# A graph network's edge loop on one core: every tile gathered, no column copies, one-hot weights by whole-group operations

## The chip, the cores and the metric

The kernel runs on one core of one Trainium2 chip. The core has five engines with instruction streams of their own: TensorE (PE, matrix products; PEld in the profile is its weight load), VectorE (DVE), ScalarE (ACT), GpSimd (POOL) and SyncE (SP, which here issues DMAs). They meet by semaphores. The metric is the device time of one execution in microseconds: 3987.03 us before the change, the median of three runs (3986.22 to 3988.06).

## The reference

One layer of attention over a graph's edges with 12,500 nodes of 64 features and 412,500 edges (400,000 and a loop for each node), sorted by receiver (dst); all in float32:

```python
h = jnp.maximum(_layernorm(x, axis=-1), 0.0)
msg_in = jnp.concatenate([h[src], h[dst], edge_attr_32], axis=-1)      # 64 + 64 + 32
messages = swish(msg_in @ W1 + b1) @ W2 + b2
att = softmax(swish(msg_in @ Wa1 + ba1) @ Wa2 + ba2, axis=0)           # over all edges
aggregated = segment_sum(messages * att, dst, num_segments=12500)
x = x + swish(concat([h, aggregated]) @ Wu1 + bu1) @ Wu2 + bu2
```

The softmax runs over all edges at once, so its maximum and its sum are known only at the end.

## The kernel before, in words

**Head.** `gnn_kernel` loads x in chunks, normalizes it, transposes it into hT (two halves of the nodes on 128 partitions), and multiplies it with the sender's and the receiver's halves of the first weights. The results are two tables in DRAM of 128 numbers per node: ts_d for senders (L274), tr_d for receivers (L310). The first gather needs all of ts_d.

**Edges.** 128 edges make a tile, K = 8 tiles make a group, and there are NG = 403 groups. `one_pass` goes over the groups. In `load(g)`, two groups ahead, GpSimd gathers the senders' rows of each tile with one indirect DMA per tile (L533) into a buffer gs, of which there are seven. SyncE loads the edge features, the receivers' numbers and a window of the receivers' table, VectorE makes one-hot columns from the receivers' numbers (L558), and four matmuls (L562) give the receivers' and the edges' share in PSUM (pe).

In 127 groups (`chosen`, every third, without the first ten and the last twelve or so) the eighth tile is not gathered. `numbers` loads its senders' numbers, `places` computes where each sender's column stands in hT (L487 to L493), `columns` copies these 128 columns one by one on ScalarE (L504, with the places in registers), and in `load` a mask (L567) and one more matmul (L568) turn them into the tile's share.

`begin(g)` adds pe and gs on VectorE (L573, written back into gs) and takes the hyperbolic tangent on ScalarE (L576). `end(g)` makes the messages (L586) and the logits (L592 to L597). For each batch of groups `top` and `weigh` update the running maximum, whose history is kept in nmax, and take the exponentials p.

**Sums by node.** Some groups later `sum_up` runs in three steps: `out_of` copies a group's sums out of PSUM (L652, ScalarE), `put` adds an earlier group's into the table sums by node (L671, L675) and notes in the table stand which maximum these sums were made with (L678), and `by_node` makes the weights wt, a one-hot row of 40 columns times p for each edge (L640, eight instructions per group), and multiplies them with the messages (L646). `project` multiplies with the update's weights (L657).

**Beside the loop** `tile_bias` and `tile_rest` make the nodes' own share of the update, one tile of nodes in eight groups; L389 adds a bias to x there.

**Tail.** After the last group the 13 tiles of nodes go through `factor` (an exponential that brings the sums to the last maximum, L830), `first`, `silu`, `second` and `rest`, and are stored. `general` is a second way for graphs whose windows are too wide; it is not taken here.

**Order.** Nearly all instructions are pinned with `pin`, so each engine keeps the order in which the program names them. SyncE, ScalarE and GpSimd issue DMAs in the order of their streams. A gather waits for the gather eight before it to have landed and for its buffer to be free.

Of the kernel before, what the change touches and what calls it, by code (L numbers as in the profile page):

```python
# [44 lines left out]
F32 = mybir.dt.float32  # L45
# [8 lines left out]
P = 128  # L54
EP = 128
# [18 lines left out]
EVERY = 3  # L74
PHASE = 1
SLOTS = (((0, 24), (24, 24)), ((48, 24), (72, 12)), ((84, 24), (108, 20)))
ROUND = 12582912.0
# [3 lines left out]
BIG = 3.0e38  # L81


PARTS = [("pair", 4 * C), ("we", C), ("bias", C), ("wu2h", 2 * D), ("wa2", U), ("bu2", D), ("w_bu", U),
         ("w2b", U), ("wu1a", U), ("wu2", D), ("ba2", 1), ("w_bup", 2 * U), ("bu1", 1)]
# [5 lines left out]
def gnn_kernel(ctx: ExitStack, tc: tile.TileContext, n_edges, x, src, src_row, dst, dst_row, first, edge,  # L91
# [14 lines left out]
    hT_d = dram.tile([2 * D, NB // 2, P], F32, name="hT_d")  # L106
# [19 lines left out]
    w_bu = part["w_bu"][:D + 1]  # L126
# [29 lines left out]
    hT = const.tile([2 * D, NB // 2, P], F32, name="hT")  # L156
# [8 lines left out]
    with tc.tile_pool(name="node1", bufs=1) as node1, \  # L165
# [7 lines left out]
        for c, n in chunks:  # L173
            xc = node.tile([P, CB, D], F32, name="xc", bufs=min(len(chunks), 8))[:, :n, :]
# [138 lines left out]
        pin(nc.scalar.dma_start(hT_d, hT))  # L313
# [6 lines left out]


def node_bias(tc, b, v, work, ps):

    nc = tc.nc
    NB, w_bu = v["NB"], v["w_bu"]
    n = min(4, NB - b)
    hb = work.tile([D + 1, 4, P], F32, name="hb")
    nc.vector.memset(hb[D:, :, :], 1.0)
    for r in range(2):
        nc.sync.dma_start(hb[:D, r:n:2, :], v["hT_d"][r * D:(r + 1) * D, b // 2:(b + n) // 2, :])  # L330
    pb = ps.tile([P, 4, P], F32, name="mt")
    nc.tensor.matmul(pb[:U, :n, :], w_bu, hb[:, :n, :], start=True, stop=True)
    return pb[:U, :n, :]
# [60 lines left out]
def one_pass(tc, n_edges, v):  # L394
# [17 lines left out]
    with ExitStack() as ctx:  # L412
# [5 lines left out]
        stand = keep.tile([P, NH + 2 * W], F32, name="stand")  # L418
# [15 lines left out]
        nc.vector.memset(start[:, 1:2], BIG)  # L434
# [5 lines left out]
        hT = v["hT"].rearrange("d b p -> d (b p)")  # L440
        stack = keep.tile([2 * D, C], F32, name="stack")
        nc.vector.tensor_tensor(stack, v["w_pair"][:, 0, :C], v["w_pair"][:, 0, C:], ALU.add)
        half = keep.tile([P, 1], F32, name="half")
        nc.vector.memset(half[:D], 0.0)
        nc.vector.memset(half[D:], 1.0)
# [10 lines left out]
        with tc.tile_pool(name="work2", bufs=2) as work2, \  # L456
# [3 lines left out]
            pes, gss, lgs, ps_, psums, sps, pps, ees, mts, nums, cols = ({} for _ in range(11))  # L460
# [10 lines left out]

            chosen = {g for g in range(8, NG - 12) if g % EVERY == PHASE}

            def numbers(g):
                if g in chosen:
                    e = (g * K + K - 1) * EP
                    n = nums[g] = small.tile([P, EP], I32, name="num", bufs=2)
                    nc.sync.dma_start(n, bass.AP(tensor=v["src_row"].tensor,
                                                 offset=v["src_row"][:, e:].offset, ap=[[0, P], [1, EP]]))

            def places(g):
                if g not in chosen:
                    return
                n = nums[g]
                near = small.tile([1, EP], F32, name="near", bufs=1)
                to = small.tile([1, EP], I32, name="to", bufs=2)
                pin(nc.vector.tensor_scalar(to, n[0:1], 1, None, op0=ALU.logical_shift_right))  # L487
                m = NB // 2
                pin(nc.vector.tensor_scalar(near, to, 1.0 / m, 0.5 / m - 0.5, op0=ALU.mult, op1=ALU.add))
                pin(nc.vector.tensor_scalar(near, near, ROUND, None, op0=ALU.add))  # L490
                pin(nc.vector.tensor_scalar(near, near, ROUND, float(1 - m * P), op0=ALU.subtract, op1=ALU.mult))
                pin(nc.vector.scalar_tensor_tensor(to, to, float(P), near, op0=ALU.mult, op1=ALU.add))
                pin(nc.vector.tensor_scalar(n, n, 1, None, op0=ALU.bitwise_and))  # L493
                cols[g] = small.tile([P, EP], F32, name="cols", bufs=2), to

            def columns(g, first, n):
                if g not in chosen:
                    return
                to, at = cols[g]
                _, regs = nc.values_load_multi_w_load_instructions(  # L500
                    at[0:1, first:first + n], engines=[ENG.Activation], min_val=0, max_val=NP // 2 - 1,
                    skip_runtime_bounds_check_because=WHY)
                for i in range(n):
                    pin(nc.scalar.copy(to[:, first + i:first + i + 1], hT[:, bass.ds(regs[i], 1)]))  # L504

            def burst(g, k):
                for i in range(EVERY):
                    columns(g + 3 + i, *SLOTS[EVERY - 1 - i][k])

# [14 lines left out]
            def load(g):  # L524
# [6 lines left out]
                for j in range(K - (g in chosen)):  # L531
                    rows = WIDE if j == 3 else EP
                    nc.gpsimd.indirect_dma_start(  # L533
                        out=full[:rows, j, :], out_offset=None, in_=ts_d[:, :],
                        in_offset=bass.IndirectOffsetOnAxis(ap=src_full[:rows, t + j:t + j + 1], axis=0))
# [25 lines left out]
                for q in range(H):  # L561
                    pin(nc.tensor.matmul(pe[:, 2 * q:2 * q + 2, :], eo[:, q * EP:(q + 1) * EP],  # L562
                                         win[:, q // 2, :, :], start=True,
                                         stop=q < H - 1 or g not in chosen))
                if g in chosen:
                    to, _ = cols[g]
                    pin(nc.vector.scalar_tensor_tensor(to, nums[g], half, to, op0=ALU.is_equal, op1=ALU.mult))  # L567
                    pin(nc.tensor.matmul(pe[:, K - 1, :], to, stack, start=False, stop=True))  # L568

            def begin(g):  # L570

                n = K - (g in chosen)
                pin(nc.vector.tensor_tensor(gss[g][:, :n, :], pes[g][:, :n, :], gss[g][:, :n, :], ALU.add))  # L573
                if n < K:
                    pin(nc.vector.tensor_copy(gss[g][:, n, :], pes[g][:, n, :]))
                pin(nc.scalar.activation(pes[g], gss[g], AF.Tanh))  # L576

            def end(g, then=None):
# [4 lines left out]
                gs, th = gss.pop(g), pes.pop(g)  # L583
# [50 lines left out]
            def by_node(g):  # L634
# [4 lines left out]
                for j in range(K):  # L639
                    pin(nc.vector.tensor_scalar(wt[:, j, :], iota_w[:EP, j // H, :],  # L640
                                                dloc[:, g * K + j:g * K + j + 1],
                                                p[:, k + j:k + j + 1],
# [498 lines left out]
```

## Time and profile before

| what | value |
|---|---|
| median of three runs | 3987.03 us |
| the profiled execution | 3986.92 us, span 3985.1 us |
| TensorE busy | 2332.9 us (59%) |
| VectorE busy | 3264.8 us (82%) |
| ScalarE busy | 2173.0 us (55%), 17,477 instructions |
| GpSimd busy | 2950.2 us (74%), 3,122 instructions |
| mean granted clock of TensorE | 0.64 |
| DMA | 391.64 MB, mean 98 GB/s |

The profile is of one execution. A group's row has the line, the engine, the operation, the tiles written and read, the shapes and the count; then the busy time and the mean duration in ns; then how long the engine was idle just before these instructions and what ended that. "issue" there means that the engine waited for nothing that the profile shows. A row of the timeline begins with the start and the duration in us; idle time before it stands in brackets. Rows of windows give each engine's busy time between two times.

### The profile page before, as it was taken

What the parts mean: (1) busy time and instruction counts of PE and PEld (TensorE: products, weight loads), DVE (VectorE), ACT (ScalarE), POOL (GpSimd) and SP (SyncE); (2) the same over time, 40 slices, a digit from 0 to 9 for tenths busy, and PEclk for the clock granted to TensorE, in tenths of its full rate; (3) what the DMA queues carried; (4) which work ended last, traced back from release to release, by engine and by line L of the source; (5) the groups of instructions that cost most, each with busy time, mean ns of one, the idle gap of its engine ahead of it and who ended that gap; (6) DMA issues with size and microseconds to landing.
All of it is one profiled execution on the core that took longest, in us unless ns stands there. A gap on an engine that the chain in (4) does not pass through costs nothing. (4 is left out here: it accounts for less than half of the span.)

```text
span 3985.1 us, 80416 instructions
## 1 busy us (share of the span) xinstructions
PE 2332.9 (59%) x11238; PEld 1888.3 (47%) x11238; DVE 3264.8 (82%) x9553; ACT 2173.0 (55%) x17477; POOL 2950.2 (74%) x3122
## 2 busy tenths in 40 slices
PE   6556566666666555555555555555655555555566
PEld 5444444454444444444444444444544444444455
DVE  6888888888888787888878888887878887878787
ACT  3655555555555555555555555555555555555512
POOL 3777777777777777777777777777777777777774
PEclk8766666666666666666666666666666665666666
DMA  8333343333333333333333333333333333333333
GB/s 287 101 99 99 95 110 92 103 99 102 102 92 95 93 85 93 87 92 88 89 94 84 95 93 86 94 84 94 88 91 94 84 95 87 91 95 84 104 105 85
DMA packets 219778, 391.64 MB, mean 98 GB/s; under 512 B 72209, under 2 KB 146898, under 8 KB 206050
## 3 DMA queue, kind: packets, MB, share of 16 engines
q0 software_dynamic: 99104, 203.16, 19.1%
q1 hardware_dynamic: 118754, 173.60, 16.7%
q10 hardware_dynamic: 1376, 9.67, 0.6%
q14 instruction: 452, 3.70, 0.3%
q8 instruction: 92, 1.51, 0.2%
HBM read 360.42 MB, written 25.72 MB: 97 GB/s over the span
## 5 line engine op out<-in xcount | busy, mean ns | idle before, releaser
L533 POOL DMA_INDIRECT gs<-ts_d,src_sb x3097 | 2933.0, 947 | 992.6 <-issue 854.1
L562 PE MATMUL pe<-wins,eo 128*128 128x256 f32 x3224 | 1465.1, 630 | 925.7 <-DVE eo L558 679.6
L504 ACT COPY cols<-hT 128x1 f32 x16256 | 1605.0, 187 | 717.7 <-issue 714.8
L562 PEld LDWEIGHTS pe<-wins,eo 128*128 128x128 f32 x3224 | 970.9, 318 | 1222.7 <-DVE eo L558 769.0
L576 ACT ACTIVATE pe<-gs 128x1024 f32<-128x1024 f32 x403 | 413.7, 1026 | 928.6 <-DVE gs L573 496.8
L573 DVE TENSOR_TENSOR gs<-pe,gs 128x1024 f32<-128x1024 f32 (+1 forms) x403 | 475.4, 1180 | 393.6 <-DMA gs<-ts_d,src_sb 369.2
L640 DVE TENSOR_SCALAR wt<-iota_w,dloc,p 128x40 f32<-128x40 f32 x3224 | 726.1, 321 | 1.8
L646 PE MATMUL sp<-wt,acts 128*65 128x40 f32 x6448 | 628.8, 268 | 6.3 <-DVE wt L640 3.9
L646 PEld LDWEIGHTS sp<-wt,acts 128*65 128x65 f32 x6448 | 589.9, 183 | 16.2 <-DVE wt L640 9.7
L657 PEld LDWEIGHTS mt<-ss,w2u 65*128 65x128 f32 x806 | 203.0, 279 | 336.2 <-issue 173.9
L657 PE MATMUL mt<-ss,w2u 65*128 65x40 f32 x806 | 181.6, 319 | 242.3 <-DVE gm L623 202.0
L616 PE MATMUL mt<-ident,mx 128*128 128x128 f32 x107 | 47.4, 443 | 445.8 <-DVE sums L675 427.2
L594 DVE TENSOR_TENSOR pe<-pe,w_all 128x512 f32<-128x512 f32 x403 | 281.8, 699 | 13.4
L558 DVE TENSOR_SCALAR eo<-dbs,bj 64x256 f32<-64x256 int32 x806 | 277.9, 375 | 18.2 <-DMA dbs<-in_dst_row_dram 9.0
L592 DVE SCALAR_TENSOR_TENSOR pe<-pe,gs 128x512 f32<-128x512 f32 x403 | 280.3, 696 | 10.5
L586 DVE SCALAR_TENSOR_TENSOR acts<-pe,gs 128x512 f32<-128x512 f32 x403 | 277.2, 688 | 12.4 <-ACT pe L576 3.2
L597 DVE TENSOR_REDUCE lg<-pe 128x8 f32<-128x512 f32 x403 | 277.0, 687 | 10.5
L616 PEld LDWEIGHTS mt<-ident,mx 128*128 128x128 f32 x107 | 19.5, 182 | 456.9 <-issue 455.0
L678 DVE COPY stand<-nmax 64x40 f32 x806 | 161.0, 200 | 3.2
L671 DVE SCALAR_TENSOR_TENSOR sums<-sums,scale,mt 64x40 f32 x214 | 54.2, 253 | 89.2 <-PE mt L657 85.0
L675 DVE TENSOR_TENSOR sums<-sums,mt 64x40 f32 x592 | 111.5, 188 | 4.7 <-PE mt L657 0.6
L357 DVE TENSOR_SCALAR bu<-mt,w_all 64x256 f32<-64x256 f32 (+1 forms) x50 | 23.9, 477 | 88.7 <-PE mt L348 88.3
(124 smaller groups left out, 1062.7 us busy)
## 6 DMA issues: line engine op xcount, KB each, us to landing
eo<-in_edge_dram SPq DMA_DIRECT2D x100, 512.0 KB
dbs<-in_dst_row_dram SPq DMA_DIRECT2D x200, 256.0 KB
gs<-ts_d,src_sb POOLq DMA_INDIRECT x3097
wins<-tr_d SPq DMA_DIRECT2D x806, 32.0 KB
num<-in_src_row_dram SPq DMA_DIRECT2D x127, 64.0 KB
ts_d<-ts SPq DMA_DIRECT2D x5, 896.0 KB
tr_d<-tr ACTq DMA_DIRECT2D x5, 896.0 KB
hT_d<-hT ACTq DMA_DIRECT2D x1, 3136.0 KB
```

The source lines that it names most:

```text
L504: pin(nc.scalar.copy(to[:, first + i:first + i + 1], hT[:, bass.ds(regs[i], 1)]))
L533: nc.gpsimd.indirect_dma_start(out=full[:rows, j, :], out_offset=None, in_=ts_d[:, :], in_offset=bass.IndirectOffsetOnAxis(ap=src_full[:ro ...
L558: pin(nc.vector.tensor_scalar(eo[:WR, e], db[:, e], bj[g // NQ % 2 * WR:(g // NQ % 2 + 1) * WR, g, h:h + 1], None, op0=ALU.is_equal))
L562: pin(nc.tensor.matmul(pe[:, 2 * q:2 * q + 2, :], eo[:, q * EP:(q + 1) * EP], win[:, q // 2, :, :], start=True, stop=q < H - 1 or g not in ...
L573: pin(nc.vector.tensor_tensor(gss[g][:, :n, :], pes[g][:, :n, :], gss[g][:, :n, :], ALU.add))
L576: pin(nc.scalar.activation(pes[g], gss[g], AF.Tanh))
L586: pin(nc.vector.scalar_tensor_tensor(acts[g % ACTS][:, :, 0:U], th[:, :, U:C], 1.0, gs[:, :, U:C], op0=ALU.add, op1=ALU.mult))
L592: pin(nc.vector.scalar_tensor_tensor(att, th[:, :, 0:U], 1.0, gs[:, :, 0:U], op0=ALU.add, op1=ALU.mult))
L594: pin(nc.vector.tensor_tensor(att, att, wa2[:EP, None, :].to_broadcast([EP, K, U]), ALU.mult))
L640: pin(nc.vector.tensor_scalar(wt[:, j, :], iota_w[:EP, j // H, :], dloc[:, g * K + j:g * K + j + 1], p[:, k + j:k + j + 1], op0=ALU.is_equ ...
L646: pin(nc.tensor.matmul(sp, acts[g % ACTS][:, j, :], wt[:, j, :], start=j == 0, stop=j == K - 1))
L657: pin(nc.tensor.matmul(pp, w2u.rearrange("s h u -> s (h u)"), sps.pop(g), start=True, stop=True))
```

## The change

- Every group gathers all eight tiles. `numbers`, `places`, `columns` and `burst` go, with the chosen groups, the input src_row, the mask and the extra matmul. ScalarE is left with tangents, exponentials and a few copies at the start.
- The sum of pe and gs goes into a buffer of its own, sm (two of them), and gs is no longer needed after that.
- The one-hot weights of a group are made by two instructions on all eight tiles, an is_equal and a multiplication, rather than by eight on one tile each.
- The copy in `out_of` goes from ScalarE to VectorE.
- stand keeps one number per node and half on 32 partitions rather than on 64, and lies in a common buffer hS with hT, in the part where the chunks of x are at the start. In the tail `factor` spreads it over the 128 partitions with a matmul with a constant matrix pick, and takes the exponential in place.
- The copy of hT to DRAM goes; the general way takes the nodes' share of the update from where the first way put it.

```diff
-SLOTS = (((0, 24), (24, 24)), ((48, 24), (72, 12)), ((84, 24), (108, 20)))
+UNSET = 1.0e30
...
-    hT = const.tile([2 * D, NB // 2, P], F32, name="hT")
+    hS = const.tile([2 * D, NP + 2 * W], F32, name="hS")
+    hT = hS[:, :NP // 2].rearrange("d (b p) -> d b p", p=P)
...
-        pin(nc.scalar.dma_start(hT_d, hT))
...
-        stand = keep.tile([P, NH + 2 * W], F32, name="stand")
+        stand = v["hS"][D:, NH:]
...
+        pick = keep.tile([P, P], F32, name="pick")
+        nc.vector.memset(pick, 0.0)
+        for h in range(2):
+            nc.vector.memset(pick[D + R * h:D + R * h + 1, h * U:(h + 1) * U], 1.0)
...
-            chosen = {g for g in range(8, NG - 12) if g % EVERY == PHASE}
...
-                for j in range(K - (g in chosen)):
+                for j in range(K):
...
-                if g in chosen:
-                    to, _ = cols[g]
-                    pin(nc.vector.scalar_tensor_tensor(to, nums[g], half, to, op0=ALU.is_equal, op1=ALU.mult))
-                    pin(nc.tensor.matmul(pe[:, K - 1, :], to, stack, start=False, stop=True))
...
-                n = K - (g in chosen)
-                pin(nc.vector.tensor_tensor(gss[g][:, :n, :], pes[g][:, :n, :], gss[g][:, :n, :], ALU.add))
-                if n < K:
-                    pin(nc.vector.tensor_copy(gss[g][:, n, :], pes[g][:, n, :]))
-                pin(nc.scalar.activation(pes[g], gss[g], AF.Tanh))
+                sm = sms[g] = work2.tile([EP, K, C], F32, name="sm", bufs=2)
+                pin(nc.vector.tensor_tensor(sm, pes[g], gss.pop(g), ALU.add))
+                pin(nc.scalar.activation(pes[g], sm, AF.Tanh))
...
-                for j in range(K):
-                    pin(nc.vector.tensor_scalar(wt[:, j, :], iota_w[:EP, j // H, :],
-                                                dloc[:, g * K + j:g * K + j + 1],
-                                                p[:, k + j:k + j + 1],
-                                                op0=ALU.is_equal, op1=ALU.mult))
+                places = dloc[:, g * K:(g + 1) * K].rearrange("p (h j) -> p h j", h=2)
+                pin(nc.vector.tensor_tensor(wt.rearrange("p (h j) w -> p h j w", h=2),
+                                            iota_w[:EP, :, None, :].to_broadcast([EP, 2, H, W]),
+                                            places[:, :, :, None].to_broadcast([EP, 2, H, W]), ALU.is_equal))
+                pin(nc.vector.tensor_tensor(wt, wt, p[:, k:k + K, None].to_broadcast([EP, K, W]), ALU.mult))
...
-                pin(nc.scalar.copy(ss, sp))
+                pin(nc.vector.tensor_copy(ss, sp))
...
-                        pin(nc.vector.tensor_copy(stand[rows, cols],
-                                                  nmax[rows, s + 1:s + 2].to_broadcast([U, W])))
+                        pin(nc.vector.tensor_copy(stand[h * R:(h + 1) * R, cells],
+                                                  nmax[h * R:(h + 1) * R, s + 1:s + 2].to_broadcast([R, W])))
...
-                burst(g, 0)
                 if g + AHEAD < NG:
                     load(g + AHEAD)
-                numbers(g + 7)
-                places(g + 6)
...
-                pin(nc.scalar.activation(fac.rearrange("u (p b) -> u p b", b=n),
-                                         fv[:, :, t * NC:t * NC + n], AF.Exp, bias=last, scale=-1.0))
+                pin(nc.tensor.matmul(fac.rearrange("u (p b) -> u p b", b=n), pick[D:],
+                                     fv[:, :, t * NC:t * NC + n], start=True, stop=True))
+                pin(nc.scalar.activation(fac, fac, AF.Exp, bias=last, scale=-1.0))
```

More of the change, by code (lines that the diff above doesn't have):

```diff
@@ L470, in one_pass @@
                 nc.vector.tensor_copy(w2u[:, h, :], w2u_ps)
-            chosen = {g for g in range(8, NG - 12) if g % EVERY == PHASE}
-            def numbers(g):
-                if g in chosen:
[L476 to L508, printed above, removed]
             at_sp, at_lo, at_hi, bus, rest = {}, {}, {}, {}, {}
@@ L910, in general @@
                        allow_small_or_imprecise_dtypes=True)
-        dst_sb = keep.tile([EP, T], I32, name="dst_g")
+        dst_sb = v["hS"][:EP, :T].bitcast(I32)
         nc.sync.dma_start(dst_sb, dst)
```

86 lines of the change are left out of this document (36 added, 50 removed).

## The prediction

> **What bounds the kernel now.** I read the page's shares, its groups, the waits, and then the timeline of single gathers. First the shares and the groups (line, engine, operation, shapes, count | busy us, mean ns | idle before it and who ended it):
>
> ```profile
> span 3985.1 us, 80416 instructions
> PE 2332.9 (59%) x11238; PEld 1888.3 (47%) x11238; DVE 3264.8 (82%) x9553; ACT 2173.0 (55%) x17477; POOL 2950.2 (74%) x3122
> ...
> L533 POOL DMA_INDIRECT gs<-ts_d,src_sb x3097 | 2933.0, 947 | 992.6 <-issue 854.1
> ...
> L504 ACT COPY cols<-hT 128x1 f32 x16256 | 1605.0, 187 | 717.7 <-issue 714.8
> ...
> L640 DVE TENSOR_SCALAR wt<-iota_w,dloc,p 128x40 f32<-128x40 f32 x3224 | 726.1, 321 | 1.8
> ```
>
> VectorE (DVE) shows the largest share, 82%, and GpSimd (POOL) only 74%. The shares mislead here. POOL's idle time is in front of its gathers, and its releaser is "issue": POOL waited for nobody. The waits and the gathers one by one (start us, duration us, and in brackets the idle time before) say the same:
>
> ```profile
> POOL gs L533 <- issue: 854.1, 2802, 0.3
> DVE gs L573 <- DMA gs<-ts_d,src_sb: 369.2, 175, 6.5
> POOL gs L533 <- DMA gs<-ts_d,src_sb: 46.9, 149, 1.8
> ...
> 49.82 1.10 POOL L533 DMA_INDIRECT gs<-ts_d,src_sb  x1 [47.43 <-DMA ts_d<-ts]
> ...
> 82.58 0.94 POOL L533 DMA_INDIRECT gs<-ts_d,src_sb  x1 [0.30 <-issue]
> 85.34 0.94 POOL L533 DMA_INDIRECT gs<-ts_d,src_sb  x1 [1.81 <-DMA gs<-ts_d,src_sb]
> ...
> 2138.29 0.94 POOL L533 DMA_INDIRECT gs<-ts_d,src_sb  x1 [0.30 <-issue]
> 2139.53 0.94 POOL L533 DMA_INDIRECT gs<-ts_d,src_sb  x1 [0.30 <-issue]
> ...
> 2148.27 0.94 POOL L533 DMA_INDIRECT gs<-ts_d,src_sb  x1 [0.30 <-issue]
> ...
> 3927.03 0.94 POOL L533 DMA_INDIRECT gs<-ts_d,src_sb  x1 [0.30 <-issue]
> ```
>
> A gather takes 0.94 us, the next follows 0.30 us later, and between the gathers POOL never rests for longer than 1.81 us (once, at 85.34). Meanwhile VectorE waits 369.2 us for rows that have not yet landed. So the kernel is a chain of gathers with a head before it and a tail behind it. The head is 49.8 us: the first gather waits for the sender table ts_d to be written. The 3097 gathers start between 49.82 and 3927.03, which is 3877.2 / 3096 = 1.2523 us each; the undisturbed stretch from 2138.29 to 2148.27 has eight in 9.98 us, 1.2475 each. The tail, from the start of the last gather to the end of the span, is 3985.1 - 3927.0 = 58.1 us. The profiled execution took 3986.92 us, 1.8 us more than its span; the median of the runs, 3987.03, is 0.1 above it.
>
> **Gathers added.** Today 127 groups (every third, from g = 10 on, with the last twelve left out) gather seven tiles, the other 276 gather eight: 127 x 7 + 276 x 8 = 3097. After the change all 403 groups gather eight: 3224, 127 more. Each sits in POOL's queue, nothing else runs there, and no slack hides it. The bounds of the interval are the two rates above. At 1.2475 us, 3223 intervals are 4020.7 us; at 1.2523 they are 4036.2 us. I take 1.2500, half way, 4028.8 us: part of what lengthens today's gathers is the work that goes (below), part stays.
>
> **Column copies removed.** 16,256 ScalarE (ACT) copies go, 1605.0 us, with the register loads between them. On VectorE the places, the mask, the add of the stacked column matmul's result and its copy go; on TensorE (PE) 127 matmuls. The loads num (SP) and the store of hT to DRAM (ACT's queue, issued after the first gather) go too. All of this lay beside POOL's chain, so I cost it at nothing. That ScalarE's stream does not slow the gathers can be seen by comparing a stretch with column copies and one behind the last chosen group, gathers alone (busy us, count, granted clock, DMA share, GB/s):
>
> ```profile
> 2000.00:2100.00 100.00, 75.62 (x81) 0.65 0.37 94
> 3800.00:3900.00 100.00, 75.62 (x81) 0.60 0.38 107
> ```
>
> 81 gathers and 75.62 us of busy POOL in both. The 1.81 us at 85.34 falls while tables are still being stored, and may go; it is inside the bounds.
>
> **Row sums in their own buffer.** The add writes sm rather than back into gs, so the gather buffer is free after the add instead of after the message and the logits. POOL's waits by releaser show 46.9 us in 149 rows for landed gathers, nearly all of them the 0.30 us that is there anyway: there is no buffer wait to remove. Cost and gain nothing.
>
> **One-hot weights by two whole-group operations.** Eight 40-column instructions per group become two of 320 columns: an is_equal whose two inputs are both in SBUF, then a multiplication whose two inputs are both in SBUF. Their duration is bounded by the same kind of instruction on 128 and 512 columns:
>
> ```profile
> L389 DVE TENSOR_TENSOR xt<-xt,w_all x13: 283/682/683, 261.1 to 1186.0; 128x512 f32<-128x512 f32 x12, 128x128 f32<-128x128 f32 x1
> ...
> L652 ACT COPY ss<-sp 65x40 f32<-65x40 f32 x403 | 73.4, 182 | 13.0 <-PE sp L646 13.0
> ```
>
> Between 283 and 682 ns, a line gives 283 + 192/384 x 399 = 0.48 us for 320 columns. 806 of them are 389 us in place of 726.1. The move of the copy ss from ScalarE to VectorE adds about 73.4 us. Even without counting what else goes, VectorE falls to 3264.8 - 726.1 + 389 + 73.4 = 3001 us, 7.4 us per group against 8 x 1.25 = 10.0 us of gathers. The time saved turns into waiting for gathers.
>
> But two SBUF inputs on VectorE hold up POOL. L389 is the only such instruction of this size in the loop today:
>
> ```profile
> 650.58 0.94 POOL L533 DMA_INDIRECT gs<-ts_d,src_sb  x1 [0.30 <-issue]
> 650.62 0.68 DVE L389 TENSOR_TENSOR xt<-xt,w_all 128x512 f32<-128x512 f32 x1
> ...
> 957.43 0.68 DVE L389 TENSOR_TENSOR xt<-xt,w_all 128x512 f32<-128x512 f32 x1
> 957.51 1.42 POOL L533 DMA_INDIRECT gs<-ts_d,src_sb  x1 [0.30 <-issue]
> ```
>
> Begun 0.08 us ahead of a gather it makes that gather 1.42 instead of 0.94 us long; begun 0.04 us behind one, it costs it nothing. The gather is thus held until about the end of the VectorE instruction: 0.48 of its 0.68 us. A 0.48 us instruction would cost at most 0.28 us, and two that follow one another can't both hit the same gather: 0 to 403 x 0.28 = 113 us. Where between? VectorE will be waiting for the last gather of each group, so its instructions keep a fixed distance from POOL's. Such a group today:
>
> ```profile
> 2140.93 1.23 DVE L573 TENSOR_TENSOR gs<-pe,gs 128x1024 f32<-128x1024 f32 x1 [3.33 <-DMA gs<-ts_d,src_sb]
> ...
> 2143.27 1.76 DVE L640 TENSOR_SCALAR wt<-iota_w,dloc,p 128x40 f32<-128x40 f32 x8
> 2143.28 0.94 POOL L533 DMA_INDIRECT gs<-ts_d,src_sb  x1 [0.30 <-issue]
> 2144.53 0.94 POOL L533 DMA_INDIRECT gs<-ts_d,src_sb  x1 [0.30 <-issue]
> ```
>
> The last gather (2138.29) leads to the add at 2140.93 and to the weights at 2143.27, 0.01 us ahead of a gather. The copy ss, now ahead of them on VectorE, moves them some 0.18 us on: the first operation would start 0.17 us behind a gather's start, the second 0.50 later, ending at about 1.15 of 1.25 us. Both miss. The margin is thin, 0.1 to 0.2 us, and groups that begin a batch carry extra small work. I take 12 us, a tenth of the bound, nearest to the rows in which L389 missed (0.94 us).
>
> A rule to weigh: the Trainium skill, page "SBUF — State Buffer", section "Who interferes with whom", says that a copy or tensor_scalar with SBUF operands can lock GpSimd out, which would make the 3224 removed tensor_scalars a burden that goes; the sum would then take 1.2475 and end near 4150. The row at 2143.28 disagrees: that gather starts under L640 and takes 0.94 us. The same section says that two SBUF inputs contend with a GpSimd instruction that reads SBUF; the 1.42 us at 957.51 agrees.
>
> **The tail.** The factor of each of the 13 output tiles becomes a matmul (64 rows, 512 columns) and an exponential in place. In the tail TensorE is full already (windows: start:end us, length, busy us of PE, its weight loads, DVE, ACT, POOL, then granted clock, DMA share, GB/s):
>
> ```profile
> 3946.00:3976.00 30.00, 25.27 (x96) 23.31 (x97) 25.54 (x51) 14.56 (x24) 15.66 (x13) 0.71 0.38 89
> ...
> 3956.64 4.27 PE L856 MATMUL pe<-w_all,gs 128*128 128x128 f32 x16
> ...
> 0.00:50.00 50.00, 35.73 (x172) 29.39 (x173) 41.14 (x58) 29.29 (x59) 1.71 (x13) 1.00 0.73 284
> ...
> 22.76 3.19 PE L270 MATMUL pn<-w_all,hT 128*128 128x256 f32 x14
> ```
>
> Of 30 us TensorE is busy 25.27, at a granted clock of 0.71; the eight matmuls of a tile take 4.27 / 2 = 2.13 us. A 256-column matmul took 3.19 / 14 = 0.23 us in the head, at a clock of 1.00, so 512 columns take 0.46 us there, and 0.64 us if scaled to the clock of 0.71. 13 x 0.64 = 8.3 us. Ends: 0, if the gaps and VectorE's 25.54 us hide it, and 12 us at twice the head's rate. I take 8. The shorter one-hot work of the last two groups, the project that now queues behind a factor matmul, and the smaller weights and copies are each under 1 us with opposite signs: nothing.
>
> **Sum.** 49.8 + 4028.8 + 58.1 + 12 + 8 = 4156.7 us of span, 1.8 around it: 4158 us. Ends: 49.8 + 4020.7 + 58.1 + 1.8 = 4130, and 49.8 + 4036.2 + 58.1 + 113 + 12 + 1.8 = 4271.
>
> **Rivals.** (1) The one-hot operations hit a gather in most groups, because the distance that I read from one group is off by 0.2 us. For it: 1.42 us at 957.51. Against: the place worked out above. Time: with half the bound, 4158 - 12 + 57 = 4203; with all of it, some 4260.
> (2) The other side: faster, because the interval between gathers shrinks when ScalarE's 16,256 copies and the short VectorE work no longer compete with POOL for issue, or because VectorE, with the largest share, was the bound after all. It decides where the interval is (3985.1 - 49.8 - 58.1 - 20) / 3223 = 1.197 us, 0.05 under any stretch quoted. At 1.18 it would give about 3933. Against it: 81 gathers per 100 us with and without the copies, and 0.30 us between gathers everywhere.
> (3) The change does nothing measurable: the 127 gathers go where POOL rests. It rests nowhere, so this needs the same 1.197 us.
> (4) The tail's matmul is hidden and the one-hot work misses: 4158 - 20 = 4138.
>
> **How the numbers follow.** Forecast with (4): 0.80, 4130 to 4195. (1): 0.17. (2) and (3): 0.03. The range 4136 to 4210 takes in most of the unknown one-hot price and leaves out the far part of (1) and all of (2). A measurement of this kernel can tell about 0.2%, 8 us, from no change; so faster 0.02, same 0.01, slower 0.97.
>
> **What would show it.** Right: 3224 gathers, starting near 50 us, at 1.25 us each; POOL still released by "issue"; VectorE's wait for gathers far above 369.2 us; ScalarE under 600 us. Wrong: gathers of 1.2 us or more in most groups, with L389's companions the new one-hot lines (rival 1); an interval under 1.2 us (rival 2); a tail much longer than 66 us, where a matmul or exponential waits in each tile; or POOL waiting for buffers.

## The result and the profile after

The changed kernel takes 4225.9 us (median of 4 runs, 4225.4 to 4226.7) against 3987.55 us for the kernel before beside it: a ratio of 1.0598, 95% interval 1.0580 to 1.0616. It is slower by 238 us; the forecast was 4158, with 4136 to 4210. On three of the chips that the experiments ran on the kernel before takes half as long again (5931 us in e5 to e8, 5925 in e9 and e10, 6031 in e15 to e17; 3986 to 3988 everywhere else), so times from these aren't compared with the others.

The page and its groups (line, engine, operation, shapes, count | busy us, mean ns | idle before it and who ended it):

```profile
span 4223.7 us, 41660 instructions
PE 2268.3 (54%) x11010; PEld 1827.9 (43%) x11010; DVE 2838.6 (67%) x6522; ACT 525.6 (12%) x818; POOL 3111.7 (74%) x3249
...
L514 DVE TENSOR_TENSOR sm<-pe,gs 128x1024 f32<-128x1024 f32 x403 | 492.9, 1223 | 999.7 <-DMA gs<-ts_d,src_sb 994.1
...
L582 DVE TENSOR_TENSOR wt<-wt,p 128x320 f32<-128x320 f32 x403 | 198.3, 492 | 13.8
L579 DVE TENSOR_TENSOR wt<-iota_w,dloc 128x320 f32<-128x320 f32 x403 | 195.9, 486 | 4.6
```

```profile
L479 POOL DMA_INDIRECT gs<-ts_d,src_sb x3224 | 3094.6, 960 | 1029.6 <-issue 950.0 <-DMA gs<-ts_d,src_sb 60.4 <-DVE lg L536 5.8
```

VectorE and ScalarE have far less to do, and the time has grown: VectorE waits 994.1 us for gathered rows, 369.2 before. POOL is still the bound. Its gathers grew from 3097 to 3224 and, on the mean, from 947 to 960 ns. The first and the last gather, by the timeline (start us, duration us):

```profile
49.66 1.10 POOL L479 DMA_INDIRECT gs<-ts_d,src_sb  x1 [47.27 <-issue]
...
4125.65 0.94 POOL L479 DMA_INDIRECT gs<-ts_d,src_sb  x1 [0.30 <-issue]
```

So the head is unchanged (49.7 us), 3223 intervals take 4076.0 us (1.2647 each, 1.2523 before), and the tail, from the last gather's start, takes 4223.7 - 4125.7 = 98.0 us, 58.1 before. I added up over all gathers, from the rows of the timeline, what each lasted beyond the undisturbed 0.9414 us (the mean of the rows up to 0.95 us), and call it the lengthening: 10.8 us before, 53.1 after. An undisturbed gather and its gap take 1.2484 us in both traces. The growth of the span, 238.6 us, is then:

| part | us |
|---|---|
| 127 more gathers, 1.2484 us each | +158.5 |
| gathers lengthened by 53.1 in place of 10.8 us | +42.3 |
| tail, 98.0 in place of 58.1 us | +40.0 |
| head and the gaps between gathers | -2.2 |

A lengthened gather, and what VectorE does beside it:

```profile
2003.35 0.95 POOL L479 DMA_INDIRECT gs<-ts_d,src_sb  x1 [0.30 <-DMA gs<-ts_d,src_sb]
...
2004.32 0.61 DVE L504 TENSOR_SCALAR eo<-dbs,bj 64x256 f32<-64x256 int32 x2
2004.60 1.14 POOL L479 DMA_INDIRECT gs<-ts_d,src_sb  x1 [0.30 <-issue]
2004.85 0.48 DVE L579 TENSOR_TENSOR wt<-iota_w,dloc 128x320 f32<-128x320 f32 x1
2005.36 0.49 DVE L582 TENSOR_TENSOR wt<-wt,p 128x320 f32<-128x320 f32 x1
2005.88 0.69 DVE L525 SCALAR_TENSOR_TENSOR acts<-pe,sm 128x512 f32<-128x512 f32 x1
2006.04 0.94 POOL L479 DMA_INDIRECT gs<-ts_d,src_sb  x1 [0.30 <-issue]
```

Of the 53.1 us, some 23 fall on gathers that start while L579 or L582 runs, and some 29 on gathers that start while L504, the operation just ahead of L579, runs. 305 gathers last over 0.96 us.

Not each operation beside a gather costs time. In the rows above L579 begins 0.25 us behind the start of the gather; of the 82 first operations (L579) that begin 0.2 to 0.35 us behind one, in 76 cases the gather is lengthened. Of the 29 that begin less than 0.2 us behind, as in the next rows, none has a lengthened gather:

```profile
1631.60 0.94 POOL L479 DMA_INDIRECT gs<-ts_d,src_sb  x1 [0.30 <-issue]
1631.70 0.49 DVE L579 TENSOR_TENSOR wt<-iota_w,dloc 128x320 f32<-128x320 f32 x1
1632.22 0.49 DVE L582 TENSOR_TENSOR wt<-wt,p 128x320 f32<-128x320 f32 x1
...
1632.85 0.94 POOL L479 DMA_INDIRECT gs<-ts_d,src_sb  x1 [0.30 <-issue]
```

In the tail, one output tile after another goes through the following (pick matmul, exponential, tanh of an earlier tile, its multiplication, its second matmuls, the next pick matmul):

```profile
4178.03 2.07 PE L766 MATMUL sp<-hS,pick 64*128 64x512 f32 x2
4180.14 0.66 ACT L768 ACTIVATE sp<-sp,nmax 128x512 f32<-128x512 f32 x1 [5.06 <-PE sp L766]
4180.72 0.59 ACT L785 ACTIVATE mt<-hS 128x512 f32<-128x512 f32 x1
4181.35 0.69 DVE L786 SCALAR_TENSOR_TENSOR hS<-mt,hS 128x512 f32<-128x512 f32 x1 [4.16 <-ACT mt L785]
...
4182.09 2.24 PE L793 MATMUL pe<-w_all,hS 128*128 128x128 f32 x8 [1.99 <-DVE hS L786]
...
4184.26 2.07 PE L766 MATMUL mt<-hS,pick 64*128 64x512 f32 x2
```

One turn takes 6.23 us. In the kernel before, the second matmuls of the thirteen tiles start between 3950.08 and 3976.03, 2.16 us a turn; here between 4150.93 and 4215.56 (the last tiles' turns are shorter), 38.7 us more, nearly all of the tail's 40. The windows of this stretch (start:end, length, busy us of PE, weight loads, VectorE, ScalarE, POOL; granted clock, DMA share, GB/s) show that no engine is full and that the granted clock is 0.50, against 0.71 in the tail of the kernel before:

```profile
4145.00:4178.00 33.00, 23.03 (x54) 12.95 (x53) 12.01 (x25) 6.90 (x12) 8.26 (x7) 0.50 0.11 27
```

### The profile page after: what moved, and what is told of

The parts are those of the page before. It is cut to its first block, busy times and chain, and to the rows that moved or that the text cites. A ratio compares the mean times of both kernels' runs of the same rounds, so it can differ in the third digit from the quotient of the medians.

```text
span 4223.7 us, 41660 instructions
## 1 busy us (share of the span) xinstructions
PE 2268.3 (54%) x11010; PEld 1827.9 (43%) x11010; DVE 2838.6 (67%) x6522; ACT 525.6 (12%) x818; POOL 3111.7 (74%) x3249
## 5 line engine op out<-in xcount | busy, mean ns | idle before, releaser
L479 POOL DMA_INDIRECT gs<-ts_d,src_sb x3224 | 3094.6, 960 | 1029.6 <-issue 950.0
L514 DVE TENSOR_TENSOR sm<-pe,gs 128x1024 f32<-128x1024 f32 x403 | 492.9, 1223 | 999.7 <-DMA gs<-ts_d,src_sb 994.1
L515 ACT ACTIVATE pe<-sm 128x1024 f32<-128x1024 f32 x403 | 414.0, 1027 | 3063.3 <-DVE sm L514 3046.2
L585 PE MATMUL sp<-wt,acts 128*65 128x40 f32 x6448 | 576.6, 259 | 23.3 <-DVE wt L582 23.3
L585 PEld LDWEIGHTS sp<-wt,acts 128*65 128x65 f32 x6448 | 544.7, 174 | 27.4 <-DVE wt L582 27.1
L531 DVE SCALAR_TENSOR_TENSOR pe<-pe,sm 128x512 f32<-128x512 f32 x403 | 282.0, 700 | 13.7
L525 DVE SCALAR_TENSOR_TENSOR acts<-pe,sm 128x512 f32<-128x512 f32 x403 | 278.7, 692 | 15.7 <-ACT pe L515 3.9
L504 DVE TENSOR_SCALAR eo<-dbs,bj 64x256 f32<-64x256 int32 x806 | 260.7, 363 | 9.0 <-DMA dbs<-in_dst_row_dram 1.4
L582 DVE TENSOR_TENSOR wt<-wt,p 128x320 f32<-128x320 f32 x403 | 198.3, 492 | 13.8
L579 DVE TENSOR_TENSOR wt<-iota_w,dloc 128x320 f32<-128x320 f32 x403 | 195.9, 486 | 4.6
L617 DVE COPY hS<-nmax 32x40 f32 x806 | 170.7, 212 | 13.5 <-issue 0.2
```

Of the source, the lines that this page charges most:

```text
L479: nc.gpsimd.indirect_dma_start(out=full[:rows, j, :], out_offset=None, in_=ts_d[:, :], in_offset=bass.IndirectOffsetOnAxis(ap=src_full[:ro ...
L504: pin(nc.vector.tensor_scalar(eo[:WR, e], db[:, e], bj[g // NQ % 2 * WR:(g // NQ % 2 + 1) * WR, g, h:h + 1], None, op0=ALU.is_equal))
L514: pin(nc.vector.tensor_tensor(sm, pes[g], gss.pop(g), ALU.add))
L515: pin(nc.scalar.activation(pes[g], sm, AF.Tanh))
L525: pin(nc.vector.scalar_tensor_tensor(acts[g % ACTS][:, :, 0:U], th[:, :, U:C], 1.0, gs[:, :, U:C], op0=ALU.add, op1=ALU.mult))
L531: pin(nc.vector.scalar_tensor_tensor(att, th[:, :, 0:U], 1.0, gs[:, :, 0:U], op0=ALU.add, op1=ALU.mult))
```

## The experiments

**All tiles gathered in the kernel before (e1).** This does the first part of the change alone.

```diff
-            chosen = {g for g in range(8, NG - 12) if g % EVERY == PHASE}
+            chosen = set()
```

> The kernel before with nothing changed but that no group is chosen: all 3224 tiles are gathered and no column is copied. Theory (POOL's chain of gathers sets the time; 127 gathers at 1.2484 us each): 3987.5 + 158.5, less some 6 us because the VectorE work of the chosen groups, which lengthens gathers, goes: 4140 us, gathers lengthened by some 5 us in all, tail 58 us. Rival (ScalarE's copies and the short VectorE work slow the gathers, so the interval shrinks without them): under 4115 us. Rival (the other parts of the change cost nothing, all of it is the gathers): 4226 us.

Measured: 4136.5 us, 1.0377 (1.0360 to 1.0394), a lengthening of 3.7 us and a tail of 56.4. The theory held. That is 150 us of the 238, the full price of the gathers (158.5) less the lengthening that left with the column work (7) and a tail shorter by 1.7. Nothing of the removed ScalarE work comes back as time.

**The factor without its matmul (e2).** The maxima stand on 128 partitions as before; the exponential reads them directly.

```diff
-        stand = v["hS"][D:, NH:]
+        stand = v["hS"][:, NH:]
...
-                pin(nc.tensor.matmul(fac.rearrange("u (p b) -> u p b", b=n), pick[D:],
-                                     fv[:, :, t * NC:t * NC + n], start=True, stop=True))
-                pin(nc.scalar.activation(fac, fac, AF.Exp, bias=last, scale=-1.0))
+                pin(nc.scalar.activation(fac.rearrange("u (p b) -> u p b", b=n),
+                                         fv[:, :, t * NC:t * NC + n], AF.Exp, bias=last, scale=-1.0))
```

> The changed kernel with the tail part undone: the table stand keeps all 64 rows of each half on 128 partitions again, and the factor is one exponential without the matmul with pick. Theory (the matmul closes a ring through PE, ACT and VectorE that passes once per tile, 6.25 us instead of 2.2): the tail goes from 98 back to some 58 us, 4226 - 40 = 4186 us, the gathers as in the changed kernel. Rival (the end of the loop, with the last sums and weights, is what grew): less than 10 us gained.

Measured: 4174.5 us, 1.0473 (1.0456 to 1.0491). The tail is 55.8 us: the pick matmul and its place account for the tail's growth. The other 10 us are gathers (lengthening 42.8 in place of 53.1). The changed kernel itself, run again (e11), had 60.5, and its gathers took 5.9 us more from first to last, so several us differ from run to run; what makes the rest of the 10 isn't shown.

**The copy ss back on ScalarE (e3).**

```diff
-                pin(nc.vector.tensor_copy(ss, sp))
+                pin(nc.scalar.copy(ss, sp))
```

> The changed kernel with the copy of the sums (ss) back on ScalarE, all else as changed. Theory (the copy moves the instructions behind it on VectorE by some 0.2 us onto the start of a gather; the second one-hot instruction of the window, L504, then starts just ahead of it, and the new one-hot weights follow): without the copy L504 ends at about 0.13 us and the weights start 0.07 us behind the start of the gather, so the gathers are lengthened by 15 to 25 us in all instead of 53: 4226 - 30 = 4196 us. Rival (the weights hit a gather wherever they stand): 4220 us or more. Rival (other places only move the blocking about): between 4210 and 4226 us.

Measured: 4226.5 us, 1.0603 (1.0585 to 1.0620), lengthening 54.3 us. The theory fell, and the first rival held. Moving VectorE's work by 0.18 us doesn't move the one-hot operations away from the gathers.

**One-hot weights tile by tile (e4).** The eight instructions of the kernel before in place of the two.

```diff
-                places = dloc[:, g * K:(g + 1) * K].rearrange("p (h j) -> p h j", h=2)
-                pin(nc.vector.tensor_tensor(wt.rearrange("p (h j) w -> p h j w", h=2),
-                                            iota_w[:EP, :, None, :].to_broadcast([EP, 2, H, W]),
-                                            places[:, :, :, None].to_broadcast([EP, 2, H, W]), ALU.is_equal))
-                pin(nc.vector.tensor_tensor(wt, wt, p[:, k:k + K, None].to_broadcast([EP, K, W]), ALU.mult))
+                for j in range(K):
+                    pin(nc.vector.tensor_scalar(wt[:, j, :], iota_w[:EP, j // H, :],
+                                                dloc[:, g * K + j:g * K + j + 1],
+                                                p[:, k + j:k + j + 1],
+                                                op0=ALU.is_equal, op1=ALU.mult))
```

> The changed kernel with the one-hot weights by eight tensor_scalar instructions per group again. Theory: what the two whole-group instructions lengthen goes (23 us), what the window's one-hot L504 lengthens stays (29 us): 4226 - 22 = 4204 us. Rival (the whole-group weights cause all of the lengthening): 4226 - 42 = 4184 us. Rival (VectorE, 0.8 us more per group, becomes the bound): over 4226 us.

Measured: 4190.3 us, 1.0512 (1.0494 to 1.0529). The theory fell, and for the gathers the first rival held. The lengthening is 8.0 us and the last gather starts at 4081.9 in place of 4125.7: the two whole-group operations cause nearly all of it, that beside L504 too (some 29 us, now 5). The tail here is 103.8 us, 6 more, for a reason that isn't shown, so the time fell by 36 and not by 44.

**One SBUF input in place of two (e6, e9, e13).** Number, size and place of the two operations stay; iota and the result of the comparison lie in PSUM.

```diff
+            bank = one_ps.tile([P, 4, P], F32, name="sp").rearrange("p a b -> p (a b)")
+            iota_p = bank[:EP, W:3 * W].rearrange("p (h w) -> p h w", h=2)
+            hit = bank[:EP, 3 * W:(3 + K) * W].rearrange("p (j w) -> p j w", j=K)
+            nc.vector.tensor_copy(iota_p, iota_w[:EP])
...
-                pin(nc.vector.tensor_tensor(wt.rearrange("p (h j) w -> p h j w", h=2),
-                                            iota_w[:EP, :, None, :].to_broadcast([EP, 2, H, W]),
+                pin(nc.vector.tensor_tensor(hit.rearrange("p (h j) w -> p h j w", h=2),
+                                            iota_p[:, :, None, :].to_broadcast([EP, 2, H, W]),
...
-                pin(nc.vector.tensor_tensor(wt, wt, p[:, k:k + K, None].to_broadcast([EP, K, W]), ALU.mult))
+                pin(nc.vector.tensor_tensor(wt, hit, p[:, k:k + K, None].to_broadcast([EP, K, W]), ALU.mult))
...
```

> The changed kernel, but the iota and the result of the comparison lie in PSUM, in the unused columns of the bank that holds the weighted sums, so that each of the two whole-group operations reads one input from SBUF and one from PSUM; their number, sizes and places stay. Theory (the gathers are lengthened because both inputs of the whole-group operations come from SBUF): the lengthening of the gathers falls from 53 us to 10 or less, the last gather starts near 4082 instead of 4126, and the time is 4180 to 4190. Rival (their length or where they fall against the gathers is the cause, whatever memory they read): the lengthening stays near 50 us and the time near 4226.

> The same kernel as in e6. Theory (two inputs from SBUF lengthen the gathers): no gather is lengthened beside the one-hot lines, the lengthening is 10 us or less in all, and where the kernel before takes 3987 us the time is 4180 to 4190, 0.990 of e11. Rival (length or place of the instructions): as e11.

In e6 and e9, on chips where the kernel before takes 5931 and 5925 us (these took 5660 and 5671), 23 and 18 gathers were over 0.96 us long, none of them beside the one-hot lines; e5 and e10, on the same chips with both inputs in SBUF, had 141 and 142. On a chip where the kernel before takes 3986 us, e13 took 4177.2 us, 1.0481 (1.0464 to 1.0499), beside 4228.6 us for the changed kernel itself (e11, 1.0610, 1.0592 to 1.0628):

```profile
L584 DVE TENSOR_TENSOR sp<-sp,dloc 128x320 f32<-128x320 f32 x403 | 201.1, 499 | 12.1
L587 DVE TENSOR_TENSOR wt<-sp,p 128x320 f32<-128x320 f32 x403 | 197.9, 491 | 13.8
```

```profile
L484 POOL DMA_INDIRECT gs<-ts_d,src_sb x3224 | 3046.0, 945 | 1030.7 <-issue 963.0 <-DMA gs<-ts_d,src_sb 25.3 <-DVE lg L541 11.6
```

```profile
2008.12 0.94 POOL L484 DMA_INDIRECT gs<-ts_d,src_sb  x1 [0.30 <-issue]
2008.22 0.50 DVE L584 TENSOR_TENSOR sp<-sp,dloc 128x320 f32<-128x320 f32 x1
2008.76 0.49 DVE L587 TENSOR_TENSOR wt<-sp,p 128x320 f32<-128x320 f32 x1
2009.37 0.94 POOL L484 DMA_INDIRECT gs<-ts_d,src_sb  x1 [0.30 <-issue]
```

The operations are as long as before (499 and 491 ns, against 486 and 492). 316 gathers start while one of them runs, with at least 0.12 us of it to go; not one is lengthened by over 0.02 us. In e11 it is 176 of 227. The gathers' busy time falls from 3094.6 (after) to 3046.0 us. The edit also moves the comparison's result into PSUM, but the multiplication still writes wt into SBUF as before, and it alone has 0 of some 238, against 109 of 148 in e11. So what lengthens a gather is the second input from SBUF, not length, place or the memory written. This is the rule that the prediction named (the Trainium skill, page "SBUF — State Buffer", section "Who interferes with whom": two SBUF inputs on VectorE contend with a GpSimd instruction that reads SBUF); 0 of 316 against 176 of 227 agrees with it.

**The order of the output loop (e5, e10, e12).** The tanh and second matmuls of tile t - 1 before the factor of tile t + 1.

```diff
-                if t + 1 < NT:
-                    factor(t + 1)
                 if 1 <= t <= NT:
                     silu(t - 1)
                     second(t - 1)
+                if t + 1 < NT:
+                    factor(t + 1)
```

> The changed kernel, but in the output loop the tanh and the second matmuls of tile t - 1 are issued ahead of the factor matmul and the exponential of tile t + 1. Theory (the tail grew because ScalarE and TensorE work in order and the factor of the next tile stands in front of the tanh and the second matmuls of the tile before, so that each tile goes once round a ring of 6.2 us): the ring opens, a tile costs TensorE its own work, 2.07 + 2.24 = 4.3 us, and 11 tiles save some 1.9 us each: the tail falls from 98.0 to about 76 us, the time from 4226 to about 4205. Rival (TensorE at its low granted clock bounds the tail by the size of its work alone): no change, 4226. Rival (the new order makes a ring of its own, with the factor now late for the scaling of its tile): slower than 4226.

> The same kernel as in e5. Theory (a ring through the in-order queues of ScalarE and TensorE): where the kernel before takes 3987 us, the tail falls from 98.0 to about 76 us and the time is 0.995 of that of e11, about 4205 us. Rival (TensorE's own work bounds the tail): as e11. Rival (a new ring): slower than e11.

Measured in e12: 4234.3 us, 1.0626 (1.0609 to 1.0644), a tail of 103.4 us. The pick matmuls follow one another at 6.50 us, as in e5 and e10, rather than 6.23:

```profile
4172.18 2.07 PE L766 MATMUL mt<-hS,pick 64*128 64x512 f32 x2
...
4174.29 0.66 ACT L768 ACTIVATE mt<-mt,nmax 128x512 f32<-128x512 f32 x1 [5.32 <-PE mt L766]
4174.88 0.59 ACT L785 ACTIVATE sp<-sm 128x512 f32<-128x512 f32 x1
...
4178.68 2.07 PE L766 MATMUL pe<-hS,pick 64*128 64x512 f32 x2
```

The expectation fell, and the edit was at fault: it moved both halves of the factor together. On ScalarE there is still an exponential right ahead of each tanh, on TensorE the second matmuls ahead of each pick, and the ring closes with one tile less of distance. The rival of a new ring held, by 6 us over e11 (4228.6). So this told a new ring from an open one, but not yet the ring from another bound.

**The ring opened (e15, e17).** Only the pick matmul goes first; the exponential comes behind the tanh. (factor has become a generator: the second next issues its matmul, the third its exponential.)

```diff
-                if t + 1 < NT:
-                    factor(t + 1)
+                ahead = factor(t + 1) if t + 1 < NT else iter((0, 0, 0))
+                next(ahead)
+                next(ahead)
                 if 1 <= t <= NT:
                     silu(t - 1)
+                next(ahead)
+                if 1 <= t <= NT:
                     second(t - 1)
```

> The changed kernel, with the output loop issued as: pick matmul of tile t + 1, tanh and multiply of tile t - 1, exponential of tile t + 1, second matmuls of tile t - 1. In e12 the exponential of tile t still stood before the tanh of tile t - 1 on ScalarE and the second matmuls of t - 1 before the pick matmul of t + 1 on TensorE, so that the ring of after (pick 2.07, exponential 0.66, tanh 0.59, multiply 0.69, second 2.24: 6.25 us) was still closed, at 6.50 us. Theory (the tail is this ring): now the tanh runs beside the pick matmul, a tile costs TensorE's own 2.07 + 2.24 us and some gaps, 4.4 us; 12 x 1.85 = 22 us less: tail 76 us, time 4204 to 4208. Rival (something else sets 6.2 us a tile): 4226 to 4229 as after. Rival (the factor comes too late for its tile's scaling, sum and tanh): 4215 or more.

> The changed kernel with both edits: the comparison's iota and result in PSUM (e13) and the output loop of e15. Theory (the two effects are independent): 51 us less from the gathers and 22 from the tail: 4155 us, that is some 20 us above the kernel before with all tiles gathered (4136.5), which is the pick matmuls' own time. Rival (ring not opened): 4177 as in e13.

Both ran on a chip where the kernel before takes 6031 us, so the times expected can't be judged (5620 and 5634 us). The output loop can be: in e5 and e10, on two other chips of this kind, it took the same 6.50 us a turn as in e12. The loop of e15, and a window of it (in the columns of the window above):

```profile
5555.02 2.07 PE L767 MATMUL pe<-hS,pick 64*128 64x512 f32 x2
...
5557.02 2.23 PE L796 MATMUL pe<-w_all,sm 128*128 128x128 f32 x8
...
5559.18 2.07 PE L767 MATMUL sp<-hS,pick 64*128 64x512 f32 x2
...
5561.19 2.23 PE L796 MATMUL pe<-w_all,hS 128*128 128x128 f32 x8
```

```profile
5541.00:5578.00 37.00, 37.00 (x90) 21.46 (x89) 18.94 (x35) 10.09 (x18) 11.71 (x10) 0.50 0.24 57
```

A tile takes 4.17 us, the two matmul groups back to back, and TensorE is busy for all of the window; the same turn in e17. The second matmuls of the thirteen tiles start within 44.2 us (5540.35 to 5584.59), against 64.6 in the changed kernel: 20 us of the 38.7 were the ring, and the other 18 are the pick matmul's own time on TensorE, at its clock of 0.50, which is now the bound of the loop. That the whole kernel gains 20 us by it was not measured on a chip where the kernel before takes 3987 us.

**Both parts undone (e7, e14).** The edits of e2 and e4 together.

> The changed kernel with both suspected parts undone: the standing maxima on 128 partitions with the factor as one exponential, and eight one-hot instructions per group. The gathers of all tiles, the sums in their own buffer and the copy on VectorE stay. Theory (the two parts hold all that the change costs beyond its 127 gathers): gathers of 1.250 us on the mean, a tail of 56 us, and 4137 us, as with all tiles gathered in the kernel before (4136.5). Rival (the new buffer of the row sums or the moved copy cost something too): 4145 or more.

> The same kernel as in e7: the factor as one exponential on 128 partitions, and eight one-hot instructions per group. Theory (these two hold all that the change costs beyond its 127 gathers): where the kernel before takes 3987 us, 4137 us, as with all tiles gathered in the kernel before. Rival (the buffer of the row sums or the moved copy cost something): 4145 or more.

In e7, beside 5931 us of the kernel before, this took 5632 us. Measured in e14: 4144.1 us, 1.0400 (1.0382 to 1.0417), lengthening 6.8 us, tail 62.0. That is 84.5 us under e11 and 7.6 above e1. The time lies just under the rival's 4145. The two parts hold nearly all; 5.6 of the 7.6 us lie in the tail (62.0 against 56.4), and their cause isn't shown.

**More column copies (e8, e16, e18).** The opposite of the change: two groups in five instead of one in three, 26 gathers fewer, 26 columns at a time.

```diff
-            chosen = {g for g in range(8, NG - 12) if g % EVERY == PHASE}
+            chosen = {g for g in range(8, NG - 12) if g % 5 in (0, 2)}
+            waiting = []
...
-                for i in range(EVERY):
-                    columns(g + 3 + i, *SLOTS[EVERY - 1 - i][k])
+                now = waiting[:26]
+                del waiting[:26]
...
+                for c in sorted({c for c, _ in now}):
+                    mine = [i for d, i in now if d == c]
+                    columns(c, mine[0], len(mine))
```

> The kernel before, but two groups in five instead of one in three gather seven tiles and take the eighth by column copies: 153 groups instead of 127, 26 gathers fewer, with the copies handed out evenly, 26 at a time. Theory (the gathers one after another are the bound and ScalarE still has room): 26 x 1.2484 = 32.5 us less, 3955 us. Rival (ScalarE, which is busy or loading registers for about 18 us per such group, becomes late: two in five make 7.3 us of column work per group of 9.5 us, and the tanh waits behind it): gathers wait for buffers and the time is 3990 or more.

> The same kernel as in e8 and e16, which fell on chips where the kernel before takes 5930 and 6031 us. Theory (one gather after another bounds the kernel before, and ScalarE has room): where it takes 3987 us, 26 x 1.2484 = 32.5 us less, 3955 us. Rival (ScalarE becomes late and holds buffers): 3990 or more. On a chip where the kernel before takes some 6000 us: again 1.15 to 1.16 of it.

In e8 and e16 this took 6835 and 6979 us, beside 5931 and 6031 us of the kernel before. Measured in e18, beside 3986.7 us of the kernel before: 5244.2 us, 1.3155 (1.3133 to 1.3177). The theory fell and the rival held, far beyond its size. The waits (us in total, times, longest):

```profile
ACT cols L506 <- issue: 2473.2, 1123, 5.4
POOL gs L539 <- issue: 2109.6, 2810, 8.1
DVE acts L592 <- ACT pe L582: 1208.5, 290, 5.9
```

The same line of the kernel before:

```profile
ACT cols L504 <- issue: 714.8, 1001, 1.7
```

ScalarE spends 2480.6 us at work and 2473.2 ahead of column copies, in all 4954 of 5242: it is the bound, and VectorE waits for its tanh. Ahead of a copy that is 0.126 us on the mean (2473.2 / 19,584), 0.044 before (714.8 / 16,256), from which I had costed it. What ScalarE does in that time, beside the register loads that stand there, the trace doesn't show; so that the kernel before could take more columns is neither shown nor excluded. No variant that ran is faster than the kernel before on a chip where that takes 3987 us.

## Why the prediction was wrong in size and right in direction

The sum gave 4156.7 us of span, and 4223.7 were measured: 35 us of the 67 lie between the first and the last gather, 32 in the tail, both in the same direction. By its own steps:

- **What bounds the kernel, and the gathers added: right.** 3224 gathers from 49.7 us on, POOL released by "issue" with no slack. 127 x 1.2484 = 158.5 us is two thirds of the loss, and e1 shows it by itself.
- **Column copies removed at nothing: right.** ScalarE fell from 2173.0 to 525.6 us and an undisturbed gather and its gap take 1.2484 us with and without them. The interval of 1.197 us that rivals 2 and 3 needed appears nowhere.
- **The buffer of the row sums at nothing: right within what e14 leaves open** (under 8 us together with the moved copy).
- **VectorE's slack turns into waiting: right**, 994.1 us. 320 columns were put at 0.48 us and took 0.486 and 0.492.
- **The one-hot operations at 12 us: right mechanism and bound, wrong place.** The gathers took 4076.0 us from first to last, 35 more than the 4028.8 + 12 forecast. The step that failed is "Both miss", and the premise under it, that VectorE's instructions keep a fixed distance from POOL's, read from a single group of the kernel before. The place that it arrived at, 0.17 us behind a gather's start, would have missed: less than 0.2 us behind cost nothing, as in the row of L389 at 650.62. But in only 29 of the 403 groups does the first operation begin there. In 82 it begins 0.2 to 0.35 us behind, in 110 it begins 0.35 to 0.45 us behind, and in 101 it begins 0.95 us or more behind, in the gap ahead of the next gather. In the median group it begins 2.8 us after the add (L514); the prediction had 2.34 and 0.18 us. 231 gathers start inside one of the two operations, with at least 0.12 us of it to go, and 165 of them are lengthened. The operations' price, 44 us by e4 and 51 by e13, lies between the ends 0 and 113 that the prediction had; rival 1, at 57 with half the bound, was nearer than the forecast. The most that one gather could lose, put at 0.28 us, was passed by 24 gathers (up to 0.38). Why the places spread so isn't shown.
- **The eight instructions on one tile each that went: next to no burden, right.** The row at 2143.28 is a weak proof, since the gather starts only 0.01 us behind L640. Whole traces are a better one: of the gathers that start well inside L640's run (0.05 us behind its start or more, with at least 0.12 us to go), 8 of 478 last over 0.96 us in e1 and 49 of 455 in the kernel before, none by over 0.1 us more than the others. In e1, which keeps all of these instructions, the lengthening of all gathers is 3.7 us together.
- **The tail at 8 us: wrong, 40 us.** Two steps failed. First the size of the matmul: "3.19 / 14" took each of the 14 instructions for a matmul, but these float32 matmuls show as two instructions each (a pick matmul, issued once, is a row with x2). At a clock of 1.00 512 columns thus cost 0.91 us. And the clock was put at 0.71, as in the tail before; the loop had 0.50, which makes 1.82 us, and they took 2.07 in place of the 0.64 forecast. The upper end of 12 us was built on the same halved figure. Second, it was added as work beside other work. It stands in a ring: pick matmul, exponential, tanh of the tile before it in ScalarE's queue, VectorE, second matmuls, next pick. e15 parts the two: 18 us are the matmul's time, 20 the ring. The prediction's list of what would prove it wrong had this case (a matmul or an exponential that waits in each tile), but its sum didn't price it.

## What to carry to other kernels

An operation on VectorE that reads two inputs from SBUF is paid for by gathers that GpSimd issues beside it; with one of the inputs in PSUM and the same size it cost nothing here (51 us less of 4229). It is not enough to read from one group where such operations fall; their places ran over nearly the whole interval between two gathers. When an operation on an in-order engine comes into a loop, write down for each queue who stands before whom and add up the ring, not only the work: 2.07 us of matmul made a tile 4.1 us longer, and a change of the order of issue gave half of it back. And before dividing a row's time by its count, check the count against the instructions that the code issues.

## What the runs showed of the hardware that was not expected

- A gather can be lengthened by an operation that begins after it. Of some 310 gathers that start while L504 runs, 132 were lengthened (some 29 us in all); with one input of the next operation in PSUM, 27 of some 300 were, 2 us in all (e13), though L504 itself is the same. How the instruction behind holds a gather already begun, and why it doesn't when it begins less than 0.2 us behind (none of 29), is not shown.
- The same program takes 3986 to 3988 us (medians) on three of the experiments' chips and 5925 to 6031 on three others, each within 0.5% on its chip. On the latter engines also stand idle where the trace names no instruction of the program that they wait for. In e7 VectorE waits ahead of one small copy (us in total, times, longest):

```profile
DVE ss L591 <- remote: 1911.7, 221, 19.1
```

  In the changed kernel's profile above the idle time ahead of this copy is some 20 us in all. On the chips of the longer times the order of the kernels turns: the variants of the changed kernel, with about half the instructions (44,007 in e7, 80,416 in the kernel before), took 0.933 to 0.958 of the time of the kernel before, and e8 and e16, with 87,481, took 1.153 and 1.159. That the engines get their instructions late there would fit these numbers, but was not tested, and the changed kernel itself was not run on such a chip.
